# A GRU's input gates as seven quarter products per four steps, with the gates' PSUM banks merged

## The chip, the cores and the metric

The kernel runs on one core of a Trainium2 chip. The metric is the device time of one execution in microseconds (us). The kernel before takes 1616.91 us, the median of 3 runs (1616.32 to 1618.04).

A core has five engines with their own instruction queues, which meet only through semaphores: TensorE (PE; its weight loads are listed as PEld), VectorE (DVE), ScalarE (ACT), GpSimd (POOL) and SyncE (SP, which issues DMAs). Matmuls write to PSUM, which has eight banks here; everything else lies in SBUF.

## The reference

Two layers with residuals, all in fp32: attention with an adaptive norm over x (16 sequences of 256 steps, 512 features), then a GRU over the 256 steps. The change concerns the GRU:

```python
def cell(h, x):
    gi = x @ W_ih + b_ih            # (16, 512) @ (512, 1536)
    gh = h @ W_hh + b_hh
    r = sigmoid(i_r + h_r)
    z = sigmoid(i_z + h_z)
    n = tanh(i_n + r * h_n)
    h_new = (1.0 - z) * n + z * h
```

`x` here is the input plus the attention's output `o + o @ W_out`. The result is that sum plus the states of the GRU. Step t+1 needs the state of step t, so the 256 steps form one chain; the input products `x @ W_ih` do not depend on the state.

## The kernel before, in words

The first 500 us or so are the attention. The rest is a loop of 256 steps over t (line 1482), which is unrolled, with the order of PE, DVE, ACT and POOL given by hand (`manual_schedule`, line 1465). What an engine waits for is put in by the tile layer from the tiles that instructions read and write.

**Layout.** A gate (16 sequences by 512 features) is computed with PE's four column groups: the 128 partitions of a gate's tile are 4 groups of 32, and the 128 columns are a quarter of the features each. With two steps (a pair) of 16 sequences a group's 32 rows are full. A matmul of one group has 32 or 16 stationary columns (the state or the inputs, transposed) and moves 128 or 256 columns of weights. `gate_part` (1054) issues four of them, one for each group; a gate's state part is `state_part` (1066), 4 chunks of k by 4 groups, 16 matmuls with `whh`.

**PSUM.** A pair p has three tiles: `gr` (r's gate and the input part of n, 256 columns; banks lg2 and A), `gn` (the state part of n; lg3 and X) and `gz` (Z and Y). Pairs alternate between the two sets (`open_gates`, 1035). The last two banks, lg0 and lg1, take the output product. `seed` (1410) copies the biases from `b_rows` into the set of the next pair, on ACT, and `input_part` (1416) adds `x @ W_ih` for both steps of the next pair: 16 matmuls of 256 columns for r and n, 16 of 128 for z.

**One step** (from 1482). PE: `state_part` for r, n and z, in this order (1493). DVE: `turned` (1422) transposes r's gate in blocks of 32 (tile trr), ACT applies the sigmoid (1500); in the first step of a pair DVE also transposes the input part of n (tri, 1502); then the gate of n (trh); n = trh * r + tri (1504, 1505), tanh on ACT (1506); the transpose trz and z's sigmoid (1508); h = (h - n) * z + n on DVE (1532 to 1534). This h is the stationary operand of the next step's state part. In even steps h is written into `padded`, whose first half is zero, so that the odd step's matmuls can use all 32 rows of a group.

**Beside the chain**, in each step: PE's share of the attention's output product (`output_step`, 1393; from group 2 of 16 steps on as seven quarter products, Strassen's scheme, in quads of four matmuls, `quarter_steps`, 1369) and of the next pair's input parts. After h: on POOL `y = x + h` (1536) and sums of operands for the quarter products (`make_o_sum`, `make_wo_sum`); on DVE the additions of finished quarter products to x (`put_quarter`, 1388), the transpose of a loaded block of 8 steps of x (`put_block`, 1308) and of a finished block of output (`store`, 1430), all of it at steps that tables give.

Of the kernel before, what the change touches and what calls it, by code (L numbers as in the profile page):

```python
# [8 lines left out]
F32 = mybir.dt.float32  # L9
AF = mybir.ActivationFunctionType  # L10
ALU = mybir.AluOpType
# [3 lines left out]
P = 128  # L15
# [5 lines left out]
def kernel(  # L21
# [99 lines left out]
    def program(ctx, bounded):  # L121
# [29 lines left out]
        def load_small():  # L151

            for j in range(4):
                bi, bh = (
                    b.rearrange("(o g j f) -> j o g f", o=1, g=3, f=P)[j].to_broadcast([32, 3, P])
                    for b in (b_ih, b_hh)
                )
                r = slice(32 * j, 32 * j + 32)
                for i, g in enumerate((0, 2, 1)):
                    nc.sync.dma_start(b_rows[r, i, :], bi[:, g, :])  # L160
                nc.sync.dma_start(b_rows[r, 3, :], bh[:, 2, :])
                nc.sync.dma_start(b_more[r], bh[:, 0:2, :])
                for q in range(KC):
                    nc.sync.dma_start(h0P[r, q, :], h0T[32 * q : 32 * q + 32, j, :])
# [499 lines left out]
        def slot2(b, w, prev, st):  # L664
# [21 lines left out]
            if b == 0:  # L686

                for c in range(KC):
                    d = wo[:, c, c * P : (c + 1) * P]
                    nc.vector.tensor_tensor(d, d, ident, ALU.add)  # L690
                load_small()
            elif b == 2:
                for i in range(2):
                    a = b_rows[:, 2 * i, :]
                    nc.vector.tensor_tensor(a, a, b_more[:, i, :], ALU.add)
# [254 lines left out]
        def quarter_slot2(b, w, prev, st):  # L950
# [23 lines left out]
            if b == 1:  # L974
                make_v_sum(T4)
            elif b == 2:
                for i in range(2):
                    a = b_rows[:, 2 * i, :]
                    nc.vector.tensor_tensor(a, a, b_more[:, i, :], ALU.add)
# [54 lines left out]

        def open_gates(p, which=(R_, N_, Z_)):

            for g, name, bank, row, n in (
                (R_, "r", ("lg2", "A")[p], 0, 2), (N_, "n", ("lg3", "X")[p], 3, 1),
                (Z_, "z", "ZY"[p], 2, 1),
            ):  # L1040
                if g not in which:
                    continue
                a = gates[g, p] = tile_ps(f"g{name}_{p}", bank, (P, n, P))
                for j in range(4):
                    nc.tensor.matmul(
                        a[32 * j : 32 * j + 32],
                        ident[:, 32 * j : 32 * j + 32],
                        b_rows[:, row : row + n, :],
                        start=True,
                        stop=True,  # L1050
                        skip_group_check=True,
                    )

        def gate_part(dst, rows, w, first, k, stationary):

            for j in range(4):
                nc.tensor.matmul(  # L1057
                    dst[32 * j : 32 * j + rows],
                    stationary,
                    w[:, k, :].rearrange("p (g j c) -> p j g c", g=3, c=P)[:, j, first::2][:, : dst.shape[1]],  # L1060
                    start=False,
# [4 lines left out]
        def state_part(t, g, hT):  # L1066

            for k in range(KC):
                gate_part(gates[g, t // 2 % 2][:, 0:1, :], hT.shape[2], whh, g, k, hT[:, k, :])

# [26 lines left out]
        def last_batch(prev):  # L1097
# [44 lines left out]
            put_turned_bank(w, 3, nc.scalar)  # L1142
            open_gates(0, (R_, N_))
            weigh(w, "A")
            put_weighed(w, nc.vector)
            open_gates(0, (Z_,))
            state_part(0, R_, h0P)
# [4 lines left out]
        def fast_last_batch(prev, st):  # L1152
# [15 lines left out]
            put_weighed_by_key(prev)  # L1168
            open_gates(0, (R_, N_))
            project_first(KC - 2)  # L1170
            open_gates(0, (Z_,))
            state_part(0, R_, h0P)
# [134 lines left out]

        def put_block(i):

            grp, half = divmod(i, TI // TG)  # L1310
            if half == 0:
                xTs[grp] = gru.tile([P, KC, TI, B], F32, tag="xT", name=f"xT_{grp}", bufs=3)
            nc.vector.transpose(
                xTs[grp][:, :, half * TG : (half + 1) * TG, :].rearrange("p q (s i) b -> p i q s b", s=2),
                xins[i],
            )
            load_block(i + 4)

# [26 lines left out]
        def make_o_sum(grp, i):  # L1345
            if i == 0:
                o_sums[grp] = gru.tile([P, 4, 2, P], F32, tag="o_sums", name=f"o_sums_{grp}")
            sums = o_sums[grp]
            a, op, c = {
# [10 lines left out]
            ("z", False, lambda g: (wo_sum(1), o_sums[g][:, 1]), (1, 0)),  # L1360
            ("q", True, lambda g: (wo_sum(2), o_sums[g][:, 0]), (1, 1)),
            ("z", False, lambda g: (wo_sum(0), o_sums[g][:, 2]), (1, 1)),
            ("q", False, lambda g: (wo_half(1, 1), o_sums[g][:, 3]), (1, 0)),
            ("z", False, lambda g: (wo_sum(3), o_half(g, 1, 1)), (0, 1)),
        )
        ADDED_AT = {1: 0, 4: 1, 7: 2, 9: 3, 10: 4, 13: 5, 15: 6}
        SUMS_AT = {2: 0, 3: 1, 5: 2, 11: 3}

        def quarter_steps(grp, unit):
            first_quad = 2 * unit - unit // 4  # L1370
            for quad in range(first_quad, first_quad + (1 if unit % 4 == 3 else 2)):
                i, km = divmod(quad, 4)
# [33 lines left out]
        def put_output(grp, m, o=None):  # L1406
            a = xTs[grp][:, m].rearrange("p t b -> p (t b)")
            nc.vector.tensor_tensor(a, o or acc["o"], a, ALU.add)

        def seed(p):  # L1410

            nc.scalar.copy(gates[R_, p % 2], b_rows[:, 0:2, :])
            nc.scalar.copy(gates[N_, p % 2][:, 0, :], b_rows[:, 3, :])
            nc.scalar.copy(gates[Z_, p % 2][:, 0, :], b_rows[:, 2, :])

        def input_part(p, g, k):

            grp, ti = divmod(2 * p, TI)
            x2 = xTs[grp][:, k, ti : ti + 2, :].rearrange("p t b -> p (t b)")
            gate_part(gates[g, p % 2], 32, wih, g, k, x2)  # L1420

# [7 lines left out]

        def store(i, y):  # L1430

            osb = gru.tile([P, TG // 2, KC, 32], F32, tag="osb", name=f"osb_{i}")
            nc.vector.transpose(osb, y.rearrange("p q (s i b) -> p i q s b", s=2, b=B))
            for j in range(4):
# [27 lines left out]

        WO_SUMS_AT = dict(zip((2, 4, 6, 7, 8, 10, 11, 12), ((i, k) for i in (0, 1, 2, 3) for k in range(2))))

        with tc.manual_schedule(engines=ORDERED):
# [11 lines left out]

            parts = [(g, k) for g in (R_, Z_) for k in range(KC)]
            for g, k in parts:
                input_part(0, g, k)  # L1480
            hT = h0P
            for t in range(T):
# [5 lines left out]
                more = 2 * p + 2 < T  # L1488
                if s == 0 and p > 0 and more:
                    seed(p + 1)  # L1490
                gr, gz, gn = (gates[g, p % 2] for g in range(3))
                if t > 0:
# [6 lines left out]
                r = tile_of("r")  # L1499
                nc.scalar.activation(r, turned("r", t, gr[:, 0, :])[:, :, s, :], AF.Sigmoid)  # L1500
                if s == 0:
                    ni = turned("i", t, gr[:, 1, :])
                n = tile_of("n")
                nc.vector.tensor_tensor(n, turned("h", t, gn[:, 0, :])[:, :, s, :], r, ALU.mult)  # L1504
                nc.vector.tensor_tensor(n, n, ni[:, :, s, :], ALU.add)  # L1505
                nc.scalar.activation(n, n, AF.Tanh)  # L1506
                z = tile_of("z")
                nc.scalar.activation(z, turned("z", t, gz[:, 0, :])[:, :, s, :], AF.Sigmoid)

                if t == 0:
                    open_gates(1)
                ready = []
                for u in range(t + 2 if t else 0, t + 3):
                    if u // TI + 1 < NI:
                        output_step(u // TI + 1, u % TI)
                        if u < TI and u % KC == KC - 1:
                            ready.append((u // TI + 1, u % TI // KC, acc["o"]))
                if more:  # L1520
                    for g, k in (parts[:3], parts[3:])[s]:
                        input_part(p + 1, g, k)

# [15 lines left out]
                if t < TI // TG:  # L1539
                    put_block(TI // TG + t)  # L1540
                for done_step in ready:
                    put_output(*done_step)
                og, unit = (t + 2) // TI + 1, (t + 2) % TI
                if 1 < og < NI and unit in ADDED_AT:
                    put_quarter(og, ADDED_AT[unit])
                if og + 1 < NI and unit in SUMS_AT:
                    make_o_sum(og + 1, SUMS_AT[unit])
                if t in WO_SUMS_AT:
                    make_wo_sum(*WO_SUMS_AT[t])
                block = t // TG + 2 * TI // TG  # L1550
                if tl == TG - 2 and block < T // TG:
                    put_block(block)
                if tl == 4 and done is not None:
                    store(*done)
                    done = None
                if tl == TG - 1:
# [39 lines left out]
```

## Time and profile before

| what | us |
|---|---|
| median of 3 runs | 1616.91 |
| the profiled execution | 1616.49 |
| its span, first to last instruction | 1614.7 |
| first transpose of a gate (step 0) | 502.85 |
| last transpose of r's gate (step 255) | 1603.55 |
| mean granted TensorE clock | 0.999 |
| VectorE busy, 1000 to 1200 us | 113.60 of 200 |
| ScalarE busy, 1000 to 1200 us | 50.72 of 200 |
| GpSimd busy, 1000 to 1200 us | 22.29 of 200 |

The profile is of one execution. Matmuls are pipelined and their ends are modelled, so PE's busy time is no measure of how full it is; how many matmuls are issued in a stretch is. In the traces an fp32 matmul instruction appears as two records: `x32` is 16 matmuls. In the text, "starts after" is the distance of two starts.

### The profile page before, as it was taken

Reading aid. Unit: us, or ns where it says so; the run is one execution under the profiler, and the core shown is the slowest. Engines: PE = TensorE matmul, PEld = TensorE weight load, DVE = VectorE, ACT = ScalarE, POOL = GpSimd, SP = SyncE. Lnnn points to the kernel's source line nnn. Section 1 sums busy time; section 2 is a strip of 40 time slices with the busy share of each in tenths; the row PEclk is TensorE's granted clock in tenths of the full one; section 3 lists DMA queues with packets and bytes.
Section 4 is the critical chain, followed back from the end, with each engine's and each line's share of the span. In section 5 each row is a group of like instructions: output and inputs, shape, how many; then the busy total and the mean of one; then the engine's idle time right before and its main releaser. Section 6 shows DMA issues by size and latency. Waiting matters only on the chain.

```text
span 1614.7 us, 103810 instructions
## 1 busy us (share of the span) xinstructions
PE 1595.5 (99%) x47606; PEld 1357.1 (84%) x47606; DVE 968.1 (60%) x3186; ACT 566.2 (35%) x1798; POOL 405.6 (25%) x726
## 2 busy tenths in 40 slices
PE   8999999999999999999999999999999999999997
PEld 5677777777767999999999999999999989999986
DVE  4777776776765555555555555555555555555554
ACT  4565665656542222222222222222222222222222
POOL 0766656566551210111101111011111101110000
PEclk9999999999999999999999999999999999999999
DMA  5100100000052000000100000100000100000000
GB/s 219 31 17 16 30 17 29 17 17 29 18 135 54 16 20 22 18 17 17 24 20 22 18 18 17 24 21 21 17 17 18 24 21 14 11 11 11 17 11 19
DMA packets 51428, 45.00 MB, mean 28 GB/s; under 512 B 10615, under 2 KB 43683, under 8 KB 50979
## 3 DMA queue, kind: packets, MB, share of 16 engines
q1 hardware_dynamic: 50889, 38.20, 8.7%
q8 instruction: 374, 6.13, 1.6%
q14 instruction: 75, 0.61, 0.1%
q10 hardware_dynamic: 90, 0.06, 0.0%
HBM read 29.79 MB, written 8.39 MB: 24 GB/s over the span
## 4 chain that ended last, share of the span: by engine, by line
PE 67%; DVE 2%; issue 1%; ACT 0%; POOL 0%; DMA 0%; DVEq 0%; ACTq 0%
PE gr L1057 27%; PE gz L1057 19%; PE gn L1057 14%; PE oz L1379 3%; PE oq L1379 2%; PE first L1018 0%; PE o L1299 0%; DVE trh L1425 0%; ACT n L1506 0%; DVE n L1504 0%; DVE n L1505 0%; PE o L779 0%; PE o L769 0%; PE lg L737 0%; POOL sums L757 0%
## 5 line engine op out<-in xcount | busy, mean ns | idle before, releaser
L1057 PE MATMUL gr<-w_a,xT 128*32 128x256 f32 x4096 | 268.2, 379 | 0.0
L1500 ACT ACTIVATE r<-trr 128x64 f32<-128x64 f32 x256 | 65.4, 256 | 504.7 <-DVE trr L1425 502.7
L1425 DVE STREAM_TRANSPOSE trr<-gr 128x128 f32<-128x128 f32 x256 | 81.1, 317 | 249.6 <-PE gr L1057 249.4
L757 POOL TENSOR_TENSOR sums<-e 128x256 f32<-128x256 f32 x240 | 168.6, 733 | 73.8 <-ACT e L751 73.8
L1506 ACT ACTIVATE n<-n 128x64 f32<-128x64 f32 x256 | 65.6, 256 | 308.9 <-DVE n L1505 305.9
L1057 PEld LDWEIGHTS gr<-w_a,xT 128*32 128x32 f32 x4096 | 129.8, 110 | 44.9
L1536 POOL TENSOR_TENSOR y<-xT,padded 128x64 f32<-128x64 f32 x128 | 40.9, 320 | 490.5 <-DVE padded L1534 490.5
L1536 POOL TENSOR_TENSOR y<-xT,h 128x64 f32<-128x64 f32 x127 | 40.4, 318 | 490.1 <-DVE h L1534 490.1
L751 ACT ACTIVATE e<-lg 128x512 f32<-128x512 f32 x256 | 131.6, 599 | 61.9 <-PE lg L737 61.9
L1425 DVE STREAM_TRANSPOSE trh<-gn 128x128 f32<-128x128 f32 x256 | 81.1, 317 | 116.6 <-PE gn L1057 116.4
L1057 PEld LDWEIGHTS gr<-w_b,padded 128*32 128x32 f32 x4096 | 115.1, 109 | 28.5 <-DVE padded L1534 27.4
L1057 PE MATMUL gr<-w_b,padded 128*32 128x128 f32 x4096 | 135.9, 273 | 2.4 <-DVE padded L1534 1.4
L1057 PE MATMUL gr<-w_b,h 128*16 128x128 f32 x4064 | 135.1, 273 | 1.2 <-DVE h L1534 0.7
L1057 PEld LDWEIGHTS gz<-w_a,xT 128*32 128x32 f32 x4096 | 117.6, 110 | 21.5
L1057 PE MATMUL gz<-w_a,xT 128*32 128x128 f32 x4096 | 135.5, 273 | 0.0
L1057 PE MATMUL gn<-w_b,padded 128*32 128x128 f32 x4096 | 135.5, 273 | 0.0
L1057 PE MATMUL gz<-w_b,padded 128*32 128x128 f32 x4096 | 135.5, 273 | 0.0
L1057 PE MATMUL gn<-w_b,h 128*16 128x128 f32 x4064 | 134.4, 273 | 0.0
L1057 PE MATMUL gz<-w_b,h 128*16 128x128 f32 x4064 | 134.4, 273 | 0.0
L1057 PEld LDWEIGHTS gz<-w_b,padded 128*32 128x32 f32 x4096 | 114.7, 110 | 0.0
L1057 PEld LDWEIGHTS gn<-w_b,padded 128*32 128x32 f32 x4096 | 114.7, 110 | 0.0
L1057 PEld LDWEIGHTS gr<-w_b,h 128*16 128x16 f32 x4064 | 105.9, 97 | 10.1 <-DVE h L1534 5.2
(196 smaller groups left out, 2749.7 us busy)
## 6 DMA issues: line engine op xcount, KB each, us to landing
xin<-in_x_dram SPq DMA_DIRECT2D x256, 32.0 KB, 2.6
out_dram<-osb SPq DMA_DIRECT2D x248, 32.0 KB, 2.5
x<-in_x_dram SPq DMA_DIRECT2D x28, 256.0 KB, 3.4
w_b<-in_L_cond_W_qkv_dram SPq DMA_DIRECT2D x4, 768.0 KB, 8.4
w_a<-in_L_cond_W_ih_dram SPq DMA_DIRECT2D x16, 192.0 KB, 5.0
w_a<-in_L_cond_W_emb_dram SPq DMA_DIRECT2D x4, 512.0 KB, 5.7
w_b<-in_L_cond_W_hh_dram SPq DMA_DIRECT2D x16, 128.0 KB, 3.0
oT<-in_x_dram SPq DMA_DIRECT2D x2, 512.0 KB, 8.7
```

The costliest lines, as they stand in the source:

```text
L751: nc.scalar.activation(w.e[i], w.lg[i], AF.Exp)
L757: nc.gpsimd.tensor_tensor(w.sums[:, i, :], w.e[i][:, 0, :], w.e[i][:, 1, :], ALU.add)
L1057: nc.tensor.matmul(dst[32 * j : 32 * j + rows], stationary, w[:, k, :].rearrange("p (g j c) -> p j g c", g=3, c=P)[:, j, first::2][:, : ds ...
L1379: nc.tensor.matmul(acc[name][32 * j : 32 * j + 32, m, :], w[:, k, j, 32 * m : 32 * m + 32], o[:, k], start=(start and km == 0), stop=(k == 1),
L1425: nc.vector.transpose(tr.rearrange("p q s b -> p (q s b)"), gate)
L1500: nc.scalar.activation(r, turned("r", t, gr[:, 0, :])[:, :, s, :], AF.Sigmoid)
L1506: nc.scalar.activation(n, n, AF.Tanh)
L1536: (nc.gpsimd if t + 1 < T else nc.vector).tensor_tensor(y[:, :, tl * B : (tl + 1) * B], xTs[grp][:, :, ti, :], h, ALU.add)
```

## The change

The first 20 steps (pairs 0 to 9) keep the old input parts. From step 20 on, `x @ W_ih` of four steps at a time (a quad; two quads share a block of 8 steps) is computed with Strassen's scheme: the rows are the two pairs of a quad, the inner dimension is halved into two pairs of k chunks, and the columns are halved into the first and second 64 of each group's 128. Seven products of 32 rows by 192 columns (three gates by 64) take the place of eight. Each product is 2 chunks by 4 groups, 8 matmuls; a unit is one chunk, four matmuls.

- **PSUM.** The products accumulate in banks Z and Y. To free these, the gate of z moves into the tile of r: `g_p` now has 3 x 128 columns (r, z and, in the first 20 steps, the input part of n), in lg2 or A; `gn_p` stays in lg3 or X. `b_rows` is reordered for this (r, z, n).
- **PE.** Step t works on quad (t+5)//4, with 4, 4, 3 and 3 units. The quads of the output product are redistributed over each four steps (2, 1, 1, 3, by the output's own count) and their due steps shift.
- **DVE.** Seven additions per quad (128x192, PSUM plus bias or plus the sum so far) build the input gates `gx` in SBUF, after h, at most two in a step. tri is transposed from `gx`. The block transposes of input and output are cut into halves at two steps.
- **ACT.** From pair 10 on `seed` copies r's and z's inputs from `gx` and n's bias, two copies in place of three, in the odd step before the pair, behind r's sigmoid.
- **POOL.** Four sums of `W_ih` quarters once (24 instructions in steps 0 to 11, two a step, and the sums for the output product behind them), four sums of input quarters per block of 8 steps. The sums of the output product's operands lie in a part of `oT` that is no longer needed.

```diff
-                for i, g in enumerate((0, 2, 1)):
-                    nc.sync.dma_start(b_rows[r, i, :], bi[:, g, :])
+                nc.sync.dma_start(b_rows[r, 0:3, :], bi)
...
-        def open_gates(p, which=(R_, N_, Z_)):
...
+        def open_gates(p):
+
+            gates[p] = (
+                tile_ps(f"g_{p}", ("lg2", "A")[p], (P, 3, P)),
+                tile_ps(f"gn_{p}", ("lg3", "X")[p], (P, 1, P)),
+            )
...
         def state_part(t, g, hT):

+            rz, hn = gates[t // 2 % 2]
+            dst = hn if g == N_ else rz[:, g : g + 1]
             for k in range(KC):
-                gate_part(gates[g, t // 2 % 2][:, 0:1, :], hT.shape[2], whh, g, k, hT[:, k, :])
+                gate_part(dst, hT.shape[2], whh, slice(g, g + 1), k, hT[:, k, :])
...
-        ADDED_AT = {1: 0, 4: 1, 7: 2, 9: 3, 10: 4, 13: 5, 15: 6}
-        SUMS_AT = {2: 0, 3: 1, 5: 2, 11: 3}
+        QUADS = (2, 1, 1, 3)
+        ADDED_AT = {3: 0, 5: 1, 7: 2, 8: 3, 11: 4, 13: 5, 15: 6}
+        SUMS_AT = {7: 0, 8: 1, 10: 2, 11: 3}
...
+        INPUTS = (
+            ("Z", True, lambda o: x_half(o, 0, 0), lambda: ih_half(0, 0)),
+            ("Y", True, lambda o: x_half(o, 0, 1), lambda: ih_half(1, 0)),
+            ("Z", False, lambda o: x_pair[o][:, S2], lambda: ih_sum(T2)),
+            ("Y", True, lambda o: x_pair[o][:, S3], lambda: ih_sum(T3)),
+            ("Z", False, lambda o: x_pair[o][:, S1], lambda: ih_sum(T1)),
+            ("Y", False, lambda o: x_half(o, 1, 1), lambda: ih_sum(T4)),
+            ("Z", False, lambda o: x_pair[o][:, S4], lambda: ih_half(1, 1)),
+        )
+        UNITS = (range(0, 4), range(4, 8), range(8, 11), range(11, 14))
+        ADDS = (
+            ((0, 0, "Z", True), (0, 0, "Y", False)),
+            ((1, 0, "Z", True), (1, 1, "Y", True)),
+            ((1, 1, "Z", False),),
+            ((1, 0, "Y", False), (0, 1, "Z", True)),
+        )
...
+        def input_units(quad, i):
+            o, q = divmod(quad, 2)
+            for unit in UNITS[i]:
+                part, k = divmod(unit, 2)
+                bank, start, stationary, w = INPUTS[part]
+                if start and k == 0:
+                    acc[bank] = tile_ps(f"in_{quad}_{part}", bank, (P, 3, 64))
+                for j in range(4):
+                    nc.tensor.matmul(
+                        acc[bank][32 * j : 32 * j + 32],
+                        stationary(o)[:, k, q],
+                        w()[:, k, j],
+                        start=(start and k == 0),
+                        stop=(k == 1),
+                        skip_group_check=True,
+                    )
+
+        def add_inputs(quad, i):
+            if i == 0:
+                for p in (2 * quad, 2 * quad + 1):
+                    gx[p] = gru.tile([P, 3, P], F32, tag="gx", name=f"gx_{p}", bufs=4)
+            for pair, half, bank, first in ADDS[i]:
+                cols = slice(64 * half, 64 * half + 64)
+                dst = gx[2 * quad + pair][:, :, cols]
+                nc.vector.tensor_tensor(dst, acc[bank], b_rows[:, 0:3, cols] if first else dst, ALU.add)
+
         def seed(p):

-            nc.scalar.copy(gates[R_, p % 2], b_rows[:, 0:2, :])
-            nc.scalar.copy(gates[N_, p % 2][:, 0, :], b_rows[:, 3, :])
-            nc.scalar.copy(gates[Z_, p % 2][:, 0, :], b_rows[:, 2, :])
+            rz, hn = gates[p % 2]
+            if p < 2 * QUAD:
+                nc.scalar.copy(rz, b_rows[:, 0:3, :])
+            else:
+                nc.scalar.copy(rz[:, 0:2, :], gx[p][:, 0:2, :])
+            nc.scalar.copy(hn[:, 0, :], b_rows[:, 3, :])
...
                 r = tile_of("r")
-                nc.scalar.activation(r, turned("r", t, gr[:, 0, :])[:, :, s, :], AF.Sigmoid)
+                nc.scalar.activation(r, turned("r", t, rz[:, R_, :])[:, :, s, :], AF.Sigmoid)
+                if s == 1 and more and p + 1 >= 2 * QUAD:
+                    seed(p + 1)
                 if s == 0:
-                    ni = turned("i", t, gr[:, 1, :])
+                    ni = turned("i", t, (rz if p < 2 * QUAD else gx[p])[:, N_, :])
...
+                if p + 1 < 2 * QUAD:
+                    for k in range(2 * s, 2 * s + 2):
+                        input_part(p + 1, k)
+                quad, part = quad_of(t)
+                quads = QUAD <= quad < T // 4
+                if quads:
+                    input_units(quad, part)
```

## The prediction

> **What bounds the kernel now.** I read the page's busy shares first, then the chain that ended last.
>
> ```profile
> PE 1595.5 (99%) x47606; PEld 1357.1 (84%) x47606; DVE 968.1 (60%) x3186; ACT 566.2 (35%) x1798; POOL 405.6 (25%) x726
> ...
> PE 67%; DVE 2%; issue 1%; ACT 0%; POOL 0%; DMA 0%; DVEq 0%; ACTq 0%
> ```
>
> By these (busy time of each engine, and the chain's shares), TensorE alone is the limit. But an average hides a second limit, so I went to the timeline. The first transpose of a step (trr) starts 256 times, the first at 502.85 us and the last at 1603.55: 1100.70 us for 255 intervals. From step 16 to step 239 the intervals repeat: 4.35 us after an even step, 4.36 or 4.17 after an odd one (two or one product quads of the output), about 68.93 for 16 steps. In the last 16 steps the output products are missing and the intervals become 4.25 and 4.16 to 4.17, and they stay so at step 254, where PE has no work beside the state's matmuls. So there is a floor, set not by PE's throughput but by the recurrence. Here it is in the timeline near the end (start us, us, engine, line, operation, tiles; in brackets idle time before it and its releaser):
>
> ```profile
> 1598.17 1.07 PE L1057 MATMUL gr<-w_b,h 128*16 128x128 f32 x32
> ...
> 1599.30 0.32 DVE L1425 STREAM_TRANSPOSE trr<-gr 128x128 f32<-128x128 f32 x1 [1.19 <-PE gr L1057]
> ...
> 1599.71 0.26 ACT L1500 ACTIVATE r<-trr 128x64 f32<-128x64 f32 x1 [2.16 <-DVE trr L1425]
> ...
> 1600.17 0.32 DVE L1425 STREAM_TRANSPOSE trh<-gn 128x128 f32<-128x128 f32 x1 [0.36 <-PE gn L1057]
> 1600.60 0.23 DVE L1504 TENSOR_TENSOR n<-trh,r 128x64 f32<-128x64 f32 x1
> 1600.86 0.22 DVE L1505 TENSOR_TENSOR n<-n,tri 128x64 f32<-128x64 f32 x1
> ...
> 1601.17 0.26 ACT L1506 ACTIVATE n<-n 128x64 f32<-128x64 f32 x1 [1.21 <-DVE n L1505]
> ...
> 1601.53 0.23 DVE L1532 TENSOR_TENSOR padded<-h,n 128x64 f32<-128x64 f32 x1 [0.17 <-ACT n L1506]
> ...
> 1602.40 0.81 PEld L1057 LDWEIGHTS gr<-w_b,padded 128*32 128x32 f32 x32 [1.70 <-DVE padded L1534]
> 1602.40 1.08 PE L1057 MATMUL gr<-w_b,padded 128*32 128x128 f32 x32 [1.42 <-DVE padded L1534]
> ```
>
> What to see: a gate's 16 matmuls issue in 0.872 us, the three gates in 2.62. trr starts 1.13 after the first matmul, so 0.26 after the last matmul of r has issued, while PE works on the next gate; trh follows 0.87 later, when gn is done; everything else hangs on trh. PE waits 1.42 us for the new state. The kernel before is thus balanced: PE about 4.26 us a step, the chain 4.2. Taking work from PE can bring at most 68.93 - 8 x (4.25 + 4.165) = 1.6 us in 16 steps; a longer chain costs in full.
>
> **The change, part by part.**
>
> *The waits of the merged banks.* This decides. In the program of before, r's, n's and z's matmuls each end in a signal of their own (after 16 matmuls, 44 or so where input parts come first), and trr, trh and trz each wait for theirs. In the program that the change builds, r and z share one tile, and PE signals once, behind the last matmul of z, a count of 48 or more. In all 256 steps trr waits for that count; trh and trz carry no wait for PE, since trr's covers them. So trr starts when 48 matmuls are done instead of 16: 2 x 0.872 = 1.744 us later, 2.875 after PE's start at an even step, 2.893 at an odd one (1.131 and 1.149 in the last steps of before).
>
> What is late next? Behind trr nothing waits for PE any more, so the legs that were covered by gn shorten. Step 0 of before shows them unwaited:
>
> ```profile
> 502.85 0.32 DVE L1425 STREAM_TRANSPOSE trr<-gr 128x128 f32<-128x128 f32 x1 [2.19 <-PE gr L1057]
> 503.09 0.28 DVE L1425 STREAM_TRANSPOSE tri<-gr 128x128 f32<-128x128 f32 x1
> 503.29 0.27 DVE L1425 STREAM_TRANSPOSE trh<-gn 128x128 f32<-128x128 f32 x1
> 505.13 0.23 DVE L1504 TENSOR_TENSOR n<-trh,r 128x64 f32<-128x64 f32 x1 [1.57 <-ACT r L1500]
> ```
>
> r starts 0.41 after trr, and n 0.29 after r's start (505.13 against 504.84): 0.70. By the other side, in an even step: tri at 0.24, trh at 0.44, done at 0.71, and 0.10 to n (as 1600.17 + 0.32 to 1600.60): 0.81. In an odd step (no tri) trh is done by 0.52, so r decides: 0.70. At most it is 0.90 (rows of 0.24 and 0.32 throughout). From n to PE's next start the last steps give 1.805 (even) and 1.74 (odd). Interval after an even step: 0.81 + 1.805 + 2.893 = 5.51. After an odd one: 0.70 + 1.74 + 2.875 = 5.32.
>
> *A second wait at the state's first matmul.* From pair 10 on ACT's seed falls into the step before, and the first matmul of an even step waits for h and for the seed. The seed is long done. The nearest row is the subtraction, which starts 0.36 after tanh where it waits for two engines, 0.29 where for one. So 0 to 0.07; I take 0.06, by that row. A pair costs 10.83, and 10.89 from step 20 on.
>
> *TensorE's work.* Now under cover. A 192-column matmul lies between 54.5 ns (128 columns) and 109 (256); by columns 82. A step has 4, 4, 3, 3 units of four and 1, 1, 3, 2 quads of 0.218: 4.14, 4.14, 4.25, 4.03 us with the state, all below 5.3. Only steps 15 to 17, which do the old input parts and the new units, come to 5.45, 5.45 and 5.56: 0.3 us over the chain. What the products save (0.65 us per four steps) is worth nothing beside the chain.
>
> *VectorE's sums.* Seven of 128x192 from PSUM per four steps; between 0.225 (64 columns) and 0.417 (256, L1391), in line 0.35; at most two in a step. They stand right after h, with at most one of: an output add (0.42), half a block transpose (0.71 / 2). At most 1.12 us, and trr is due 2.9 after h ends (0.06 to PE's start, 2.875 from there). Hidden; without cover, 2.5 us per four steps.
>
> *ACT.* The seed (0.37 and 0.26) now stands between r and tanh: r ends 0.67 after trr, both copies issue by 1.14 (0.30 and 0.20 apart in the rows of before), tanh is due at 1.28. Nothing, at most 0.1 in odd steps.
>
> *POOL and SP.* 24 weight sums (256 columns, 0.73) at two a step up to step 11, first read at step 16; four x sums of 128 columns per eight steps, between 0.32 and 0.73, read a step or more later; y waits behind them and nobody waits for y but a store. SP issues eight small loads fewer; a block's load is issued one step later, more than eight before it is read. Zero each.
>
> *The sum.* Step 0: 5.26 + 1.74 = 7.0. Steps 1 to 19: 9.5 pairs x 10.83 = 102.9. Steps 20 to 254: 117.5 x 10.89 = 1279.6. Steps 15 to 17: 0.3. Together 1389.8, against 1100.7: +289.1. Ahead, the first trr waits for z's input part too: +0.9. Behind, trr to n shrinks from 1.29 to 0.70 in the last step: -0.6. Sum +289.4 on the profiled execution's 1616.5 (span 1614.7 and 1.8 around): **1906**. The median shown, 1616.9, is 0.4 above that execution, which changes nothing.
>
> [...] trr of before reads r's bank while PE writes gn's, and the trace shows no delay in either. [...]
>
> **Rivals.**
>
> 1. *The wait does not bite, and the products pay* (faster). If trr started on r's own end, four steps would take 4.17, 4.25, 4.25 and 4.25 = 16.92 against 17.23, 55 times: -17.1; steps 15 to 17 give back 3.6, a second wait in the odd intervals that the chain sets 3 at most. About **1604**. It decides if trr's wait is met within 1.74 us of PE's start. Against it: the only signal stands behind z. 4 in 100.
> 2. *PE's longer pauses cost clock.* PE would pause 1.2 us in every step. If the granted clock fell to the 0.83 that the last 8 us of before show, the state's 2.62 would become 3.16: +0.54 x 255 = 138, **2044**. Against it: at 1598 to 1602, with PE idle for 1.06 of 4 us, the granted clock is 1.00. 4 in 100.
> 3. *The sums are the price*: trr as before, but VectorE's sums uncovered, 2.5 us x 59 - 17 + 3.6 = +134, **1751**. Against it: VectorE is free for 1.20 us ahead of trr even at the floor (as at 1603.55), and 1.12 is the most that is needed. 2 in 100.
>
> **How the numbers follow.** The forecast has 90 in 100. Its unknowns: n by the r path in even steps (-14) or by the longest rows (+12), no second wait (-7), ACT's seed on the chain (+12), the signal's leg 0.05 off (±13). Added as independent, about ±25: **1880 to 1932**; it leaves out the rivals and some of the forecast's own error, 2 in 10. Slower by over 0.2% (which is about what a measurement can tell from no change): 95; within: 1; faster: 4.
>
> **What would show it.** Intervals between trr of 5.5 and 5.3 us, alternating; trr 2.9 us after the state's first matmul, with PE on the input products by then; TensorE's share of the span near 85% (256 steps of some 4.4 busy in 5.4) and the chain of waits no longer almost all PE; PE waiting over 1 us for h in every step. Wrong would be trr within 1.2 us of PE's start, a granted clock below 0.98, or trr waiting for VectorE's own sums.

## The result, and the profile after

The changed kernel takes **1919.2 us**, the median of 6 runs (1915.58 to 1920.85), beside 1616.88 for the kernel before (6 runs, 1616.32 to 1618.32). The ratio is 1.186, with a 95% interval of 1.185 to 1.188: slower by 302 us. The forecast was 1906, with a range of 1880 to 1932. The profiled execution took 1920.85, its span is 1919.1 and its mean granted clock 0.994.

From the page of the changed kernel, the same two lines as were shown of before (busy time of each engine; the chain's shares):

```profile
PE 1610.1 (84%) x46326; PEld 1344.7 (70%) x46326; DVE 1039.9 (54%) x3662; ACT 534.3 (28%) x1672; POOL 473.6 (25%) x870
...
PE 40%; DVE 22%; issue 6%; ACT 5%; DVEq 1%; ACTq 0%; POOL 0%
```

TensorE has 1280 records fewer than before (46326 against 47606), and its share of the span falls from 99 to 84%. The chain that ended last, two thirds PE and hardly anything else before, now runs through VectorE and ScalarE for 27% of the span. So PE is no longer the limit. The recurrence is, and the timeline of one even step shows why (start us, us, engine, line, operation, tiles; in brackets idle time before it and its releaser):

```profile
1192.72 1.07 PE L1054 MATMUL g<-w_b,h 128*16 128x128 f32 x32 [0.97 <-DVE h L1639]
...
1195.59 0.32 DVE L1516 STREAM_TRANSPOSE trr<-g 128x128 f32<-128x128 f32 x1 [2.42 <-PE g L1054]
...
1195.83 0.27 DVE L1516 STREAM_TRANSPOSE tri<-gx 128x128 f32<-128x128 f32 x1
1196.00 0.26 ACT L1599 ACTIVATE r<-trr 128x64 f32<-128x64 f32 x1 [4.05 <-DVE trr L1516]
1196.03 0.27 DVE L1516 STREAM_TRANSPOSE trh<-gn 128x128 f32<-128x128 f32 x1
...
1196.40 0.23 DVE L1605 TENSOR_TENSOR n<-trh,r 128x64 f32<-128x64 f32 x1
...
1198.21 1.08 PE L1054 MATMUL g<-w_b,padded 128*32 128x128 f32 x32 [1.26 <-DVE padded L1639]
```

Read it from the top. PE begins the state part at 1192.72. trr, which needs r alone, starts at 1195.59, 2.87 later, when r, n and z are all done; VectorE has stood idle for 2.42 us until then. From there the three transposes run one behind the other without a wait, n starts 0.81 after trr, and PE starts again 1.81 after n. The sum is 5.49, where the same path took 4.23 at the end of before (1598.17 to 1602.40 in the prediction's rows). PE's work of the step was done early: it waits 1.26 us for the new state.

Over the whole loop, trr starts first at 505.16 and last at 1908.90: 1403.74 for 255 intervals, against 1100.70 before and 1389.8 in the forecast. The median interval from step 20 on is 5.51 after an even step and 5.40 after an odd one (forecast 5.51 and 5.38).

### The profile page after: what moved, and what is told of

It reads as the page before. It is cut to its first block, busy times and chain, and to the rows that moved or that the text cites. A ratio compares the mean times of both kernels' runs of the same rounds, so it can differ in the third digit from the quotient of the medians.

```text
span 1919.1 us, 102014 instructions
## 1 busy us (share of the span) xinstructions
PE 1610.1 (84%) x46326; PEld 1344.7 (70%) x46326; DVE 1039.9 (54%) x3662; ACT 534.3 (28%) x1672; POOL 473.6 (25%) x870
## 4 chain that ended last, share of the span: by engine, by line
PE 40%; DVE 22%; issue 6%; ACT 5%; DVEq 1%; ACTq 0%; POOL 0%
PE g L1054 27%; PE gn L1054 12%; DVE trr L1516 4%; ACT n L1607 3%; DVE n L1605 3%; DVE n L1606 3%; ACT r L1599 2%; DVE padded L1638 2%; DVE padded L1639 2%; DVE h L1638 2%; DVE h L1639 2%; DVE padded L1637 2%; DVE h L1637 2%; DVE trh L1516 1%; DVE tri L1516 1%
## 5 line engine op out<-in xcount | busy, mean ns | idle before, releaser
L1054 PE MATMUL g<-w_b,padded 128*32 128x128 f32 x8192 | 275.4, 275 | 158.9 <-DVE padded L1639 158.9
L1516 DVE STREAM_TRANSPOSE trr<-g 128x128 f32<-128x128 f32 x256 | 81.1, 317 | 571.1 <-PE g L1054 571.1
L1054 PE MATMUL g<-w_b,h 128*16 128x128 f32 x8128 | 274.4, 274 | 133.5 <-DVE h L1639 132.3
L1054 PEld LDWEIGHTS g<-w_b,padded 128*32 128x32 f32 x8192 | 219.8, 110 | 195.6 <-DVE padded L1639 192.7
L1054 PEld LDWEIGHTS g<-w_b,h 128*16 128x16 f32 x8128 | 219.1, 97 | 166.3 <-ACT z L1609 155.3
L1480 PE MATMUL in<-ih_sums,x_pair 128*32 128x192 f32 x2832 | 137.9, 326 | 0.0
L1054 PEld LDWEIGHTS gn<-w_b,h 128*16 128x16 f32 x4064 | 115.5, 98 | 0.2
L1480 PEld LDWEIGHTS in<-ih_sums,x_pair 128*32 128x32 f32 x2832 | 95.7, 110 | 11.2 <-issue 0.6
L1480 PE MATMUL in<-w_a,xT 128*32 128x192 f32 x1888 | 87.5, 326 | 0.0
L1516 DVE STREAM_TRANSPOSE trz<-g 128x128 f32<-128x128 f32 x256 | 79.0, 309 | 0.0
```

What stands on the lines that cost most here:

```text
L1054: nc.tensor.matmul(dst[32 * j : 32 * j + rows], stationary, w[:, k, :].rearrange("p (g j c) -> p j g c", g=3, c=P)[:, j, which], start=Fal ...
L1480: nc.tensor.matmul(acc[bank][32 * j : 32 * j + 32], stationary(o)[:, k, q], w()[:, k, j], start=(start and k == 0), stop=(k == 1), skip_gr ...
L1516: nc.vector.transpose(tr.rearrange("p q s b -> p (q s b)"), gate)
```

## The experiments

Four statements had to be tested. The texts on record use their letters.

- **W**, the theory: trr waits for a signal that comes behind the last matmul of the shared tile, so the place of z's matmuls sets the interval.
- **S**, the rival: other new work, VectorE's sums above all, holds the pace.
- **C**: where PE is idle for more than half of a step, its granted clock falls (for the last steps of the changed kernel).
- **D**: an instruction with two semaphore waits starts some 0.06 us later than one with a single wait, even if the other was met long ago.

The last two came from differences between the trace and the forecast. Times below are medians of 4 to 11 runs; ratios are against the kernel before, run on the same chip.

**1. z's matmuls ahead of n's** (`e1_order_rzn`). One line of the changed kernel:

```diff
-                    for g in (R_, N_, Z_):
+                    for g in (R_, Z_, N_):
```

> The changed kernel with the state's matmuls issued r, z, h_n instead of r, h_n, z; nothing else. Theory W (r's transpose waits for the signal behind the last matmul of the tile that r shares with z): that signal now comes after 32 matmuls, r's transpose starts 2.0 us after the state's first matmul, and the transpose of h_n, at 2.9, is late next; from there 0.42 to n. Intervals 5.12 and 5.12 us instead of 5.51 and 5.40, 86 us less: about 1833 us. Theory S (VectorE's sums or any other part of the change holds the pace): the order of the gates changes nothing, 1919 us.

Measured: 1834.44 us (1833.24 to 1835.77), ratio 1.1345 [1.1326, 1.1364]. The median intervals are 5.12 and 5.12. The timeline of the experiment:

```profile
1191.84 1.94 PE L1054 MATMUL g<-w_b,h 128*16 128x128 f32 x64 [0.68 <-DVE h L1639]
...
1193.83 0.32 DVE L1516 STREAM_TRANSPOSE trr<-g 128x128 f32<-128x128 f32 x1 [1.54 <-PE g L1054]
...
1194.71 0.32 DVE L1516 STREAM_TRANSPOSE trh<-gn 128x128 f32<-128x128 f32 x1 [0.36 <-PE gn L1054]
```

trr now starts 1.99 after PE's start instead of 2.87: the 32 matmuls of r and z (x64 records) come first, and 16 of them are worth 0.88. trh has a wait of its own again, for gn. The amount of work is unchanged, only the place of the last matmul into the shared tile moved, and 85 us went with it. W is confirmed and S, as the main cause, is refuted.

**2. The merge alone, in the kernel before** (`e2_merge_only`). z's gate moves into r's tile; input parts, sums and output quads stay as they were.

```diff
-                (R_, "r", ("lg2", "A")[p], 0, 2), (N_, "n", ("lg3", "X")[p], 3, 1),
+                (R_, "r", ("lg2", "A")[p], 0, 3), (N_, "n", ("lg3", "X")[p], 3, 1),
...
-                if g not in which:
+                if g not in which or g == Z_:
                     continue
...
+                if g == R_:
+                    gates[R_, p], gates[Z_, p] = a[:, 0:2], a[:, 2:3]
```

> The kernel before with one edit: z's gate lies in the tile and bank of r and the input part of n; the input parts stay as eight eighths on TensorE, no quarter products, no sums on VectorE. Theory W: the merge alone brings the loss, intervals 5.51 and 5.32 us as TensorE's 4.36 is under cover: about 1898 us. Theory S: the merge costs nothing, 1617 us.

Measured: 1880.53 us (1877.52 to 1880.8), ratio 1.1628 [1.1608, 1.1647]. From its timeline, an even step:

```profile
1195.85 1.07 PE L1059 MATMUL gr<-w_b,h 128*16 128x128 f32 x32 [0.85 <-DVE h L1536]
...
1198.73 0.32 DVE L1427 STREAM_TRANSPOSE trr<-gr 128x128 f32<-128x128 f32 x1 [2.94 <-PE gr L1059]
...
1199.08 0.26 ACT L1502 ACTIVATE r<-trr 128x64 f32<-128x64 f32 x1 [3.24 <-DVE trr L1427]
```

trr starts 2.88 after PE's start, as in the changed kernel. So the merge by itself costs 264 of the 302 us. The intervals are 5.46 and 5.20, below the 5.51 and 5.32 that W gave. The difference lies in two rows: r starts 0.35 after trr here (0.41 in the changed kernel), tanh 0.26 after the addition in even steps (0.32). In this kernel's instructions those two carry one semaphore wait, in the changed kernel two. That led to D.

**3. r, i and h_n in one tile, z alone** (`e3_rn_tile`). The changed kernel with another pair of gates merged, and three seeds in place of two:

```diff
-                tile_ps(f"gn_{p}", ("lg3", "X")[p], (P, 1, P)),
+                tile_ps(f"gz_{p}", ("lg3", "X")[p], (P, 1, P)),
...
-            dst = hn if g == N_ else rz[:, g : g + 1]
+            rn, zt = gates[t // 2 % 2]
+            dst = {R_: rn[:, 0:1], N_: rn[:, 2:3], Z_: zt}[g]
```

> The changed kernel with another pairing of the gates: r, the input part of n and h_n share a tile, z has the other. Quarter products and sums as they are; three copies in place of two seed a pair. Theory W: the signal comes after 32 matmuls and covers all that n needs; r's transpose at 2.02 us, n 0.70 to 0.81 later; intervals 4.63 and 4.60 us: about 1700 us (1690 to 1710). Theory S: 1919 us.

Measured: 1675.89 us (1675.44 to 1677.16), ratio 1.0365 [1.0347, 1.0382]; intervals 4.58 and 4.45. trr waits for 32 matmuls, as in experiment 1, but z's 16 now run behind them, beside the chain. Again the time is below what was expected, by 24 us, and again r and tanh carry one wait each.

**4. Each sum twice** (`e4_sums_twice`). A copy of every addition to `gx`, into a spare tile, added ahead of it:

```diff
+                spare_sum = gru.tile([P, 3, 64], F32, tag="spare_sum", name=f"spare_{quad}_{pair}_{half}_{bank}")
+                nc.vector.tensor_tensor(spare_sum, acc[bank], b_rows[:, 0:3, cols], ALU.add)
                 nc.vector.tensor_tensor(dst, acc[bank], b_rows[:, 0:3, cols] if first else dst, ALU.add)
```

> The changed kernel with every addition of a quarter product on VectorE done a second time, into a tile that nobody reads (seven more 128x192 additions per four steps, 413 in all). Theory W: they stand between h and r's transpose, where VectorE has 2.9 us to spare, so nothing changes: 1919 us, within 5. Theory S: each costs its 0.35 us or the 0.27 that it takes in a row, 110 to 145 us: 2029 to 2064 us.

Measured: 1919.9 us (1918.09 to 1920.81), ratio 1.1868 [1.1848, 1.1887], with the same median intervals as the changed kernel. Some 80 us more of VectorE's time cost nothing: the sums are hidden, and S falls.

**5. One wait each** (`e5_one_wait`). The seed of r and z as two copies, and a matmul of 16 columns by zeros, one step early, which adds nothing. By the first, ScalarE already waits for its own earlier copy, and its later instructions need no second wait for it; by the second, PE has met the seed's signal before the state's first matmul comes.

```diff
-                nc.scalar.copy(rz[:, 0:2, :], gx[p][:, 0:2, :])
+                for g in (R_, Z_):
+                    nc.scalar.copy(rz[:, g, :], gx[p][:, g, :])
...
+                if s == 1 and more and p + 1 >= 2 * QUAD:
+                    nc.tensor.matmul(
+                        gates[(p + 1) % 2][0][0:B, 0, 0:B], zeros, ident[:, 0:B],
+                        start=False, stop=True, skip_group_check=True,
+                    )
```

> The changed kernel with its three tied gates, but with ACT and PE made to see two old signals early: the seed of r and z is two copies of 128 columns (the second waits for the first), and a matmul of 16 columns with zero weights into the next pair's tile, behind the odd step's products, waits for the seed. After that r's sigmoid, tanh and the state's first matmul wait for one semaphore instead of two. Theory D (a second wait ahead of an instruction costs 0.06 us even where it is long met): tanh and the odd step's r come 0.06 earlier each, PE at an even step 0.06 to 0.08; intervals 5.45 and 5.22 instead of 5.51 and 5.40, 28 us less, about 1891 us. Rival: those 0.06 are no cost of waiting, and only the tail of the change's own cost stands: 1919 us, or some us more for the added instructions.

Measured: 1890.11 us (1888.68 to 1890.44), ratio 1.1688 [1.1672, 1.1704]; intervals 5.45 and 5.24. More instructions, and 29 us less. From its timeline, an even step:

```profile
1192.35 0.32 DVE L1517 STREAM_TRANSPOSE trr<-g 128x128 f32<-128x128 f32 x1 [1.86 <-PE g L1054]
1192.59 0.27 DVE L1517 STREAM_TRANSPOSE tri<-gx 128x128 f32<-128x128 f32 x1
1192.70 0.26 ACT L1602 ACTIVATE r<-trr 128x64 f32<-128x64 f32 x1 [4.31 <-DVE trr L1517]
```

r starts 0.35 after trr, not 0.41 as in the first fence of this part. D holds, with a price of 0.06 us on ScalarE. The trace agrees: in the changed kernel a semaphore instruction that waits for trr stands 0.06 us ahead of r (1195.94 and 1196.00), and ScalarE has 108 of these from 1100 to 1300 us; in this experiment and in experiment 2 it has none there.

**6. PE kept busy in the last steps** (`e6_busy_tail`). Six 128x128 identity matmuls into bank Z in steps 251 to 254 of the changed kernel, whose results nobody reads:

```diff
+                if T - 6 < t < T - 1:
+                    warm_up("Z", 6)
```

> The changed kernel with six matmuls of the identity with itself, into a free bank, in each of the steps 251 to 254, which have no input or output products left. Theory C (TensorE's granted clock falls there because PE is idle more than half of the time, and this makes these intervals 7.0 to 7.5 us instead of 5.4 to 5.5): the clock stays at 1.00 and the four intervals return to 5.5 and 5.4, 6.7 us less: about 1912.5 us. Rival: the last steps are long for another reason, and nothing changes: 1919 us.

Measured: 1912.96 us (1912.38 to 1913.69), ratio 1.1832 [1.1815, 1.1848]. The windows at the end show what it did (window; PE, PEld, DVE, ACT and POOL busy with their records; granted PE clock; DMA share; GB/s). First the changed kernel:

```profile
1870.00:1880.00 10.00, 6.68 (x224) 5.88 (x220) 4.58 (x20) 1.85 (x8) 0.64 (x2) 1.00 0.01 3
1880.00:1885.00 5.00, 2.41 (x67) 2.17 (x60) 1.87 (x8) 1.20 (x5) 0.32 (x1) 0.87 0.00 0
1885.00:1890.00 5.00, 2.42 (x51) 2.13 (x41) 1.69 (x8) 0.74 (x3) 0.00 (x0) 0.79 0.02 3
1890.00:1895.00 5.00, 4.48 (x96) 3.95 (x96) 0.73 (x3) 0.00 (x0) 0.32 (x1) 0.66 0.22 49
```

Then the experiment, at the same steps:

```profile
1880.00:1885.00 5.00, 3.94 (x107) 3.57 (x106) 1.65 (x9) 0.81 (x5) 0.32 (x1) 1.00 0.01 3
1885.00:1890.00 5.00, 3.49 (x101) 3.30 (x104) 1.93 (x9) 0.66 (x3) 0.33 (x1) 1.00 0.09 21
```

In the changed kernel the last input products end in step 250, and those of the output before that. PE then has 2.6 us of work in 5.5, and the mean granted clock of a window falls from 1.00 to as little as 0.66: in the window from 1890, 96 records keep PE "busy" for 4.48 us, because a gate's 16 matmuls take up to 1.98 us in these steps instead of 1.07. With useless work in the gaps the clock stays at 1.00 and three of the last four intervals are 5.5 and 5.4 again (one is 0.37 longer). C holds for these steps: 6 us.

**7. r, z and h_n in a tile each** (`e7_three_tiles`). From pair 10 on the sets need not alternate so far ahead, as the inputs come from `gx`: r takes the tile of set 0, z that of set 1, and z is seeded behind its own sigmoid. Before that z keeps banks Z and Y up to pair 7, and is merged in pairs 8 and 9 alone.

```diff
+        def gates_of(p):
+
+            a, hn = gates[p % 2]
+            if p < MERGED:
+                return a[:, 0:1], z_alone[p % 2], hn
+            if p < 10:
+                return a[:, 0:1], a[:, 1:2], hn
+            return gates[0][0][:, 0:1], gates[1][0][:, 0:1], hn
...
-            dst = hn if g == N_ else rz[:, g : g + 1]
+            dst = gates_of(t // 2)[g]
...
-                nc.scalar.copy(rz[:, 0:2, :], gx[p][:, 0:2, :])
+                nc.scalar.copy(r[:, 0, :], gx[p][:, 0, :])
...
+                if s == 1 and more and p + 1 >= 2 * QUAD:
+                    nc.scalar.copy(gates_of(p + 1)[Z_][:, 0, :], gx[p + 1][:, Z_, :])
```

> The changed kernel with tiles of their own for r, z and h_n again: in pairs 0 to 7 z lies in Z and Y as before the change, pairs 8 and 9 stay merged, and from pair 10 on r always uses the first set's tile and z the second's, since the inputs now come by ACT's copies and need no tile in advance; z's copy follows z's sigmoid. Quarter products and sums as in the change. Theory W: r's transpose waits for r alone, the chain is at its floor again, 4.23 and 4.25 us with the second wait, and the products of TensorE fit beside it (4.14, 4.14, 4.25, 4.03): 16.98 instead of 17.23 for four steps, 14 us less than before the change, 6 back in steps 15 to 19: about 1609 us (1603 to 1616). Theory S in its weak form (with steps of 4.2 us again the sums, 1.12 us where 1.20 is free, delay r's transpose and n): 0.1 to 0.3 us a step more, 1635 to 1680 us.

Measured: 1620.23 us (1617.78 to 1623.35, 11 runs), ratio 1.0023 [1.0014, 1.0032]: the quarter products are in and 299 of the 302 us are gone. Still it is not the expected 1609. Four intervals sum to 17.0 at the median, near the 16.92 that rival 1 worked out, against 17.23 before; but some 40 steps are 0.1 us or more above the median of their place in the four, 12.6 us together, where before has 8 such steps and 2.1 us. The longest, in PE's timeline:

```profile
1225.96 0.86 PE L1079 MATMUL g<-w_b,h 128*16 128x128 f32 x24
1227.85 0.30 PE L1079 MATMUL g<-w_b,h 128*16 128x128 f32 x3 [1.03 <-issue]
```

PE stops for 1.03 us in the midst of z's 16 matmuls, and waits for nothing that the profile shows. There are 11 such stops of more than 0.15 us from 520 to 1600 us, 4.2 us together. Experiment 3 has 5, 1.8 us together; before, the changed kernel and the next experiment have none. The last section says where they fall; what causes them wasn't tested.

**8. Three tiles and one wait each** (`e8_three_one_wait`). Experiment 7 with the edits of experiment 5: r's seed in two halves and the matmul by zeros.

```diff
-                nc.scalar.copy(r[:, 0, :], gx[p][:, 0, :])
+                for c in (slice(0, 64), slice(64, P)):
+                    nc.scalar.copy(r[:, 0, c], gx[p][:, 0, c])
```

> The kernel with three tiles (as in the run before it) with r's seed as two copies of 64 columns and the zero matmul of 16 columns, so that r's sigmoid, tanh and the state's first matmul wait for one semaphore. Theory D: the floor falls by 0.12 us a step to 4.05 and 4.13, below TensorE's own 4.17, 4.14, 4.28, 4.03; four steps take 16.72: 28 us less than before the change, 6 back: about 1595 us (1588 to 1604). Rival (the second wait costs nothing): as the run before it, about 1609 us.

Measured: **1602.08 us** (1601.35 to 1602.96), ratio 0.991 [0.9896, 0.9923], faster than both kernels by more than the measurement's uncertainty. From its page and then its timeline:

```profile
PE 1572.8 (98%) x46834; PEld 1358.4 (85%) x46834; DVE 1086.4 (68%) x3662; ACT 570.2 (36%) x1914; POOL 473.7 (30%) x871
...
PE 67%; DVE 2%; issue 1%; ACT 1%; POOL 0%; DVEq 0%; ACTq 0%
```

```profile
1192.62 1.08 PE L1079 MATMUL g<-w_b,padded 128*32 128x128 f32 x32
...
1193.77 0.32 DVE L1550 STREAM_TRANSPOSE trr<-g 128x128 f32<-128x128 f32 x1 [0.32 <-PE g L1079]
```

trr is back at 1.15 after PE's start, PE at 98%, and the chain's shares are those of the kernel before. Four intervals take 3 x 4.19 + 4.30 = 16.87, against 17.23 before and 16.72 expected. The 4.30 belongs to the step with three units and three quads, for which 4.28 was expected. What the expectation had wrong is mainly the even steps, 4.19 where it had 4.14 and 4.13: there PE starts 0.28 after h's last addition starts, so the chain sets them. In the last steps, which have no products, the chain takes 4.19 after an even step and 4.10 after an odd one, against 4.25 and 4.24 in experiment 7: the even interval fell by tanh's 0.06 alone, and not by 0.12.

r and z in one bank, but as two tiles with a wait each, was not tried: VectorE would read the bank while TensorE writes it, and what comes of that was not shown here.

## Why the prediction was right, point by point

The mechanism, the place and the size were right; the time came out 13 us above the forecast, inside the range.

- *The kernel before is balanced between PE and the chain.* Right: with the chain lengthened by 0.9 us a step or more, all PE's saving was lost (the changed kernel and experiment 1), and with the chain restored, PE's saving came back (8). The 4.26 that the prediction gives for PE's step should be 68.93 / 16 = 4.31; the sum does not use it.
- *trr waits for 48 matmuls instead of 16, 1.744 us later.* Right: 2.87 and 2.90 after PE's start, 2.875 and 2.893 in the forecast. Experiment 1 moved it by the 0.872 of one gate.
- *n follows trr after 0.81 or 0.70.* Right in both: 1195.59 to 1196.40 above, and 1201.11 to 1201.81 in the odd step after it, where the trace names r as what n waited for.
- *PE's next start 1.805 or 1.74 after n.* Right: 1.81 in the step shown. The even interval came out at 5.51, exactly.
- *A second wait at the state's first matmul, 0.06.* Right in kind, slightly small. It is 0.09: PE starts 0.37 after h's last addition starts (1192.35 to 1192.72), 0.28 where it has one wait. The odd interval is 5.40 for 5.38, which is 2.3 us over the loop. Missed was that r and tanh had second waits as well; they lay in the rows that the forecast used, so they did not spoil the sum, but they explain why experiments 2 and 3 came out lower than it would have them.
- *PE's work is under cover, apart from 0.3 us in steps 15 to 17.* Right: these take 5.43, 5.52 and 5.55.
- *VectorE's sums are hidden.* Right: 0.349 us each (0.35 in the forecast), and twice as many cost nothing (4).
- *ScalarE's seed costs nothing, POOL and SP nothing.* ScalarE's seed: right in the step at 1201, where both copies (1201.68 and 1201.98) are done before tanh at 1202.38. For POOL and SP no run took them away; nothing in the chain's shares speaks against it.
- *The first trr 0.9 later.* It came 2.3 later in this execution; in experiments 1, 5 and 6, with the same steps up to there, it came 0.9 to 1.0 later, in experiment 4 2.4. The rest arises in the attention, ahead of the change: a matmul of `lg` that starts at 474.79 before and at 474.84 in experiment 6 starts at 476.25 here.
- *Step 0, 7.0 us.* Right.

**What was missed** makes up the 13.9 us between the 1389.8 forecast for the 255 intervals and the 1403.74 measured. The last four intervals, which the clock stretched, are 6.7. 22 short pauses of 0.1 to 0.36 in steps 20 to 250 are 4.7; the kernel before has 8, 2.1 us. The odd interval gives 2.3; the remaining 0.2 is in the first 20 steps. The first two are no terms of the stated range: that they fitted into it is owed to the terms that it does count, which came out near nothing, and is partly luck. Of the 302 us, the merge alone makes 264 (2), the second waits 29 (5) and the clock of the last steps 6 (6).

**The rivals.** Rival 2, the clock, had the right mechanism at the wrong place. With PE busy 8.61 of 10 us (700 to 710) the granted clock is 1.00, and still with 6.68 of 10 (1870 to 1880); in the loop it falls only in the last steps, where PE is busy 2.41 of 5 (1880 to 1885, clock 0.87), so it cost 6.7 us and not 138. The forecast had looked for it in the last steps of before, where PE is idle for 1.06 of 4 us, and not in the last steps of the changed kernel, which have no products left. Rival 3, the sums, did not occur (4). Rival 1, that the wait does not bite, did not occur either, but its price for four steps was sound: 16.92, where experiment 7, which takes the wait away, has 17.0. That its 1604 us in all is near the 1602 of experiment 8 is partly luck: experiment 8 also takes three second waits away, and experiment 7, without that, took 1620 with its pauses.

## What to carry to other kernels

When two results of one engine are put into one tile, look up which signal their first reader waits for: here it became the last write into the tile, and a reader that had been 0.26 us behind its data was 2.0 behind. On a chain that is as long as the bottleneck's work, that delay counts in every step, less the waits that it covers (here trr came 1.74 us later, and the chain grew by 1.2 to 1.3), while what the merge was to make room for counts only down to the chain's length. If a merge can't be avoided, merge the results that are produced next to each other and read at the same time, and put them first: experiment 3 did so with r, i and h_n and took 1675.89 us, where the changed kernel took 1919.2.

## What the runs showed of the hardware beyond that

**A second wait had a price here though it was met long ago.** One on each of r, tanh and the state's first matmul cost 0.06, 0.06 and 0.09 us; without them a pair of steps was 0.22 shorter (10.91 to 10.69) and the kernel 29 us faster, with more instructions in it (5 against the changed kernel). That is tanh's 0.06 in the even step, and r's and PE's in the odd one; there tanh gains only 0.01, since the seed's third copy, begun at 1198.81 in experiment 5, stands before it at 1199.01.

**In the last steps the clock fell to half, in stretches of 3.41 us.** In the changed kernel's last steps the pauses ahead of the state part are 2.6 to 3.0 us, and a gate's 16 matmuls take 1.68 to 1.98 us in place of 1.07 while the clock is down. Windows cut where the clock changes show when it falls (columns as in experiment 6):

```profile
1876.84:1880.25 3.41, 2.73 (x96) 2.56 (x96) 1.37 (x6) 0.00 (x0) 0.32 (x1) 1.00 0.02 5
1880.25:1883.66 3.41, 0.82 (x32) 0.75 (x32) 1.87 (x8) 1.20 (x5) 0.32 (x1) 1.00 0.00 0
1883.67:1887.07 3.40, 3.40 (x74) 3.40 (x68) 0.00 (x0) 0.00 (x0) 0.00 (x0) 0.50 0.02 5
1887.08:1890.49 3.41, 0.37 (x16) 0.09 (x8) 2.14 (x10) 0.74 (x3) 0.01 (x1) 1.00 0.01 2
1890.50:1893.90 3.40, 3.40 (x68) 3.14 (x72) 0.26 (x1) 0.00 (x0) 0.30 (x1) 0.50 0.22 48
```

From 1883.67 to 1907.55 the clock stands at 0.50 and 1.00 by turns, 3.41 us each; the window means of 0.66 to 0.87 are mixtures of the two. Each of the four stretches at 0.50 follows one of 3.41 us in which PE was busy for only 0.37 to 1.15 us. A stretch with 1.70 (1808.57 to 1811.98) and pauses of 1.6 and 1.7 (at 1872.03 and 1877.52) left the clock at 1.00. PE was not idle throughout the stretches ahead of a fall: what fell together with the clock is PE's share of a stretch.

**Short pauses went with the place in the instruction stream.** Steps 118, 127, 154 and 180 are 0.14 to 0.36 longer than the median in the changed kernel and in experiments 1, 3, 5, 6, 7 and 8, but not in experiment 4, which gives VectorE more instructions. In the changed kernel's step 118 VectorE waits 0.46 us ahead of h's multiplication, behind an instruction of its own. Counting each engine's instructions in the traces, semaphore instructions included, shows an order: the 11 stops of PE in experiment 7 lie whole multiples of 256 instructions apart (weight loads counted), and each of the 22 pauses of the changed kernel, the 20 of experiment 4 and the 8 of before holds a late start at one and the same place of every 256 instructions on PE, or of every 128 on VectorE and ScalarE. In the changed kernel VectorE's records 2623, 2751 and 3135 (steps 118, 127 and 154; counted from 0, each 63 more than a multiple of 128) start 0.40 us after the record ahead of them has ended, in place of 0.04 (2623 and 2751) and 0.12 (3135) at the median. Most such places have no pause: its steps 20 to 250 hold 248 of them on PE, 26 on VectorE and 12 on ScalarE. What the engines do there, and why experiment 7 has the most, wasn't tested.
